# Weighted values a step later, inverses between GpSimd's folds: another order in a local attention loop

## The chip, the core and the metric

The kernel runs on one core of a Trainium2 chip. The metric is the device time of one execution in microseconds (us), the median of several runs; lower is better. All data are float32 unless said otherwise.

## The reference

A transformer block on x of 2 x 2048 x 256: attention with 16 heads of 16 in which each position sees itself and the 64 before it, a layer norm, a feed-forward layer in which each token goes to one of eight experts, and two more norms.

```python
qkv = x @ W_attn + b_attn                     # heads of 16
scores = einsum('bhtd,bhsd->bhts', q, k) * scale
mask = causal & (j >= i - 64)
attn = softmax(where(mask, scores, -inf), axis=-1)
out = einsum('bhts,bhsd->bhtd', attn, v)
x = layernorm(x + out @ W_proj + b_proj)

expert_idx = argmax(x @ Wr.T)                 # one expert of 8 for each token
inter = gelu(x @ W1[e] + b1[e])               # e = the token's expert
y = layernorm(inter @ Wo + bo + x) * gamma + beta
x = layernorm(x + y)
```

## The kernel before

The 4096 tokens are 32 tiles of 128. The first part of the kernel (to about 312 us of the span) is a loop over the tiles with one step for each tile; the second part runs the experts over blocks of 128 tokens that were sorted by expert, with gathered rows. The change lies in the first part and in the few lines that close it.

The order of the instructions on each engine is the order in which the program writes them: the loop is written out inside a manual schedule for TensorE, VectorE, ScalarE, GpSimd and the DMA queue of SyncE. Each engine works strictly down its own list, and semaphores that the tile framework sets hold an instruction back until its data are there, or until a buffer that it writes has been read.

A step `i` works on four tiles at once, each at another stage: `t = i`, `u = i - 1`, `w = i - 2`, `z = i - 3`.

- For `t`: `scores` (TensorE, L526 and L538) adds the mask and the products of queries and keys into four PSUM banks `s0` to `s3` of four heads each. `row_max` (VectorE, L550) takes each row's maximum of a bank, `exps` (ScalarE, L554) the exponentials, four instructions for each bank, into `pr`. `fold` (GpSimd, L566) adds the two halves of two banks' rows; with its second call it goes on to fold the sums in place three times, to widths 32, 16 and 8 (L574). The scores of the next step write the same four banks again.
- For `u`: `turn` (TensorE, L609) transposes the exponentials, a bank at a time, and `keep_turned` copies them out of PSUM into `pT`: banks 0 and 2 on ScalarE (L615), banks 1 and 3 on VectorE (L617). `pT` has one buffer. `weigh` (TensorE, L629, 64 matmuls) multiplies them with the values (`v` and `h`, the same values shifted by half a tile), and `keep_weighed` (ScalarE, L639) copies the result `pa` into `av`.
- For `w`: `inverse` (VectorE, L582 and L587) ends the row sums and inverts them, `spread_inverse` (GpSimd, L595) widens them to `rw`, `turn_inverse` (TensorE, L648) transposes that into PSUM, `normalise` (VectorE, L652) multiplies `av` with it, and `join` projects (TensorE, L660), adds the residual and takes the norm's statistics (VectorE, L666 to L670).
- For `z`: `norm_scale` (GpSimd, L676 and L677), `norm` (VectorE, L685, with the store to DRAM on SP's queue, L688), `turn_x1` (TensorE, L698) and `keep_x1` (ScalarE, L703). Every fourth step `route` (L710) and `turn_logits` (L720) take the router's logits of four tiles.

Between these stand two slots for the projection of later chunks of four tiles (`project`, L415 to L426, and `keep`, L462 to L492), by a table `work`; by it the steps repeat with a period of four (counted by `i` modulo 4). GpSimd adds the output bias to the residual at some steps (`add_bias`, L1111), and VectorE gets routing work at others.

Two kinds of PSUM buffers matter. Projections and `pa` share two banks in rotation (`psum`). All that is transposed, and `join`'s product, shares two others, taken in turn in the order of the calls:

```python
def turned(name):
    turns.append(name)
    return ps_t.tile([P, 4, P], F32, tag=f"pt{len(turns) % 2}", name=name)
```

so each such product waits until the one before the last has been read.

Of the kernel before, what the change touches and what calls it, by code (L numbers as in the profile page):

```python
# [17 lines left out]
P = 128  # L18
# [15 lines left out]
def kernel(  # L34
# [250 lines left out]
    with ExitStack() as att:  # L285
# [260 lines left out]
        def row_max(i, r):  # L546
            if r == 0:
                probs[i] = p2.tile([P, 4, 4, P], F32, tag="pr", name=f"pr_{i}", bufs=3)
                maxes[i] = small.tile([P, 4, 4], F32, tag="nm", name=f"nm_{i}")
            nc.vector.tensor_reduce(maxes[i][:, r, :], banks[i][r], AX.X, ALU.max, negate=True)  # L550

        def exps(i, r):
            for x in range(4):
                nc.scalar.activation(  # L554
                    probs[i][:, r, x, :], banks[i][r][:, x, :], AF.Exp,
                    bias=maxes[i][:, r, x : x + 1], scale=1.0,
                )

        def fold(i, pair):

            pr = probs[i]
            if pair == 0:
                sums[i] = p2.tile([P, NH, P // 2], F32, tag="fd", name=f"fd_{i}")
            fd = sums[i]
            two = slice(2 * pair, 2 * pair + 2)
            nc.gpsimd.tensor_tensor(  # L566
                fd[:, 8 * pair : 8 * pair + 8, :],
                pr[:, two, :, 0:CTX].rearrange("p r x c -> p (r x) c"),
                pr[:, two, :, CTX:P].rearrange("p r x c -> p (r x) c"), ALU.add,
            )  # L570
            if pair == 1:
                n = P // 4
                while n >= 8:
                    nc.gpsimd.tensor_tensor(  # L574
                        fd[:, :, 0:n], fd[:, :, 0:n], fd[:, :, n : 2 * n], ALU.add
                    )
                    n //= 2

        def inverse(i):

# [9 lines left out]
        def spread_inverse(i):  # L590

            ri = rTs.pop(i)
            rw = p2.tile([P, KC, 4, 2, HD], F32, tag="rw", name=f"rw_{i}")

            nc.gpsimd.tensor_copy(  # L595
                rw.rearrange("p g r o d -> p r g o d"),
                ri.rearrange("p (r g o) -> p r g o", r=4, g=KC).unsqueeze(4).to_broadcast(
                    [P, 4, KC, 2, HD]
                ),
            )  # L600
            rTs[i] = rw

        def turn(i, r):

            if r == 0:
                pTs[i] = p2.tile([P, 4, 4, P], F32, tag="pT", name=f"pT_{i}", bufs=1)
            pt = turned(f"pt_{i}_{r}")
            for x in range(4):
                nc.tensor.transpose(pt[:, x, :], probs[i][:, r, x, :], ident)  # L609
            pts[i, r] = pt  # L610
# [40 lines left out]
        def normalise(i):  # L651
            nc.vector.tensor_tensor(avs[i], avs[i], rTs.pop(i)[:, 0:KC, :], ALU.mult)  # L652
# [52 lines left out]
        def route(c):  # L705

            pl = turned(f"pl_{c}")
            for k in range(KC):
                for j in range(TPC):
                    nc.tensor.matmul(  # L710
                        pl[32 * j : 32 * j + 32, 0, :], lhsT=wrT[:, k, :], rhs=x1Ts[c][:, j, k, :],
                        start=(k == 0), stop=(k == KC - 1),
                    )
            lT = p2.tile([P, P], F32, tag="lT", name=f"lT_{c}", bufs=1)
            nc.scalar.copy(lT, pl[:, 0, :])
            x1Ts[c] = lT
# [484 lines left out]
        for i in range(NT):  # L1201


            t, u, w, z = (n if n >= 0 else None for n in range(i, i - 4, -1))
            slots = work[i]
            if w is not None:
                inverse(w)
            scores(t)
            if z is not None and z > 0 and z % TPC == 0:
                route(z // TPC - 1)  # L1210
            row_max(t, 0)
            if i == 0:
                consts = routing_constants()
                for r in range(1, 4):
                    row_max(t, r)
                for r in range(2):
                    exps(t, r)
                for n in ((0, 3), (1, 0), (1, 1)):
                    prepare(*n)
                for part in ((0, 3, 0), (0, 3, 1), (1, 0, 0), (1, 0, 1)):  # L1220
                    project(*part)
                    keep(*part)
                add_bias(0)
                xts[2] = load_x(2)
                for r in range(2, 4):
                    exps(t, r)
                for part in parts[:2]:
                    project(*part)
                    keep(*part)
                for pair in range(2):  # L1230
                    fold(t, pair)
                continue
            if i == 3:
                turn_router()
            if u is not None:
                turn(u, 0)
                keep_turned(u, 0)
                turn(u, 1)
            if z is not None:
                norm_scale(z)  # L1240
            if w is not None:
                spread_inverse(w)
            for part in slots:
                if part and part[2] == 0 and part[3][0] == 0:
                    prepare(*part[:2])
            exps(t, 0)
            row_max(t, 1)
            if u is not None:
                keep_turned(u, 1)

            full = slots[0] and slots[1] and slots[0][1] > 0 and slots[0][3] == (0, 1)
            if full:
                for task in early.get(i, ()):
                    task()
            if slots[0]:
                project(*slots[0])
            if i >= TPC + 3 and (i - 3) % TPC == 0:
                turn_logits((i - 3) // TPC - 1)

            light = not slots[0] or slots[0][3] == (0,)  # L1260
            if not light:
                exps(t, 1)
            row_max(t, 2)
            if slots[0]:
                row_max(t, 3)
            if u is not None:
                turn(u, 2)
                keep_turned(u, 2)
            if light:
                exps(t, 1)  # L1270
            if t < NT - 1:
                fold(t, 0)
            if i >= TPC - 1 and i % TPC in (0, TPC - 1):
                c = (i + 1) // TPC
                if c < NT // TPC:
                    add_bias(c, 2, 2 if i % TPC == 0 else 0)
                if i % TPC == 0 and c + 2 < NT // TPC:
                    xts[c + 2] = load_x(c + 2)
            for task in spread.get(i, ()):
                task()  # L1280
            if u is not None:
                turn(u, 3)
                keep_turned(u, 3)
            if not slots[0]:
                row_max(t, 3)
            if slots[0] and slots[0][3][-1] == 1:
                keep(*slots[0][:3])
            if z is not None:
                norm(z)
            exps(t, 2)  # L1290
            if slots[1]:
                project(*slots[1][:4])
            if w is not None:
                turn_inverse(w)
                normalise(w)
            if t == NT - 1:
                for b in range(2):
                    gather(b)
                inverse(u)
                spread_inverse(u)  # L1300
                quick_sums(t, 0)
            if not full:
                for task in early.get(i, ()):
                    task()
            if slots[1] and len(slots[1]) > 4:
                keep(*slots[1][:4])
            elif slots[1] and slots[1][3][-1] == 1:
                keep(*slots[1][:3])
            if u is not None:
                weigh(u)  # L1310
            exps(t, 3)
            if t < NT - 1:
                fold(t, 1)
            if u is not None:
                keep_weighed(u)
            if i == NT - 2:
                table(0)
            if z is not None:
                turn_x1(z)
                keep_x1(z)  # L1320

            if i == TPC:
                load_experts()
            if i == 2 * TPC:
                turn_biases()
            for task in plan.get(i, ()):
                task()
            if t == NT - 1:
                quick_sums(t, 1)
            if w is not None:  # L1330
                join(w)

# [5 lines left out]
            load_weights(n // PIECES, n % PIECES)  # L1340
        turn_in(0)
        keep_in(0)
        turn(u, 0)
        keep_turned(u, 0)
        turn(u, 1)
# [231 lines left out]
```

## Time and profile before

| | |
|---|---|
| runs | 584.68, 584.70, 584.93 us; median 584.7 |
| profiled execution | 585.55 us, span of its trace 583.7 us |
| TensorE clock granted, mean | 0.992 |
| busy in the span, us | TensorE 555.0, weight loads 452.0, VectorE 402.4, ScalarE 301.6, GpSimd 408.0 |
| busy from 120 to 150 us, of 30 | TensorE 29.65, weight loads 21.73, VectorE 26.69, ScalarE 20.91, GpSimd 22.06 |
| `exps` (L554) | 512 instructions, 142.2 us |
| `fold`, first adds (L566) | 62, 79.0 us |
| `fold`, in place (L574) | 93, 76.3 us |
| `keep_weighed` (L639) | 32, 372 to 523 ns |
| `norm` (L685) | 32, 328 to 1303 ns |

In the rows of the timeline the columns are the start in us from the span's start, the busy time in us, engine, line, operation, what is written and read with shapes, the number of instructions, and in brackets the engine's idle time before it with what ended it. PE is TensorE and PEld its weight loads, DVE VectorE, ACT ScalarE, POOL GpSimd, SP SyncE. Rows of one line that follow each other closely are merged into one. The ends of matmuls are modelled; their starts are recorded.

### The profile page before, as it was taken

How to read it: one execution, taken by the hardware profiler on the slowest of the kernel's cores; microseconds unless marked ns; L12 is line 12 of the kernel's file. 1: busy time of each engine (PE TensorE's matmuls, PEld its weight loads, DVE VectorE, ACT ScalarE, POOL GpSimd, SP SyncE). 2: the span in 40 equal slices, each digit the busy share in tenths (PEclk: the TensorE clock that was granted, in tenths of full speed). 3: DMA queues.
4: the chain of work that ended last, by engine and by line, in shares of the span. 5: the costliest groups of instructions: out<-in, count | busy, mean ns of one | idle time of the engine just before them, and what ended most of it. 6: DMA issues, size and time to landing. Idle time of an engine off the chain costs nothing.

```text
span 583.7 us, 18527 instructions
## 1 busy us (share of the span) xinstructions
PE 555.0 (95%) x7312; PEld 452.0 (77%) x7312; DVE 402.4 (69%) x966; ACT 301.6 (52%) x1005; POOL 408.0 (70%) x603
## 2 busy tenths in 40 slices
PE   8999999999999999999898999999999999999990
PEld 5658667676776767766666898999999999999880
DVE  5659788888988889989877567887863332232582
ACT  2487675776758577576765433233335455455100
POOL 5359777677787887868973488887878677652483
PEclk9999999999999999999999999999999999999996
DMA  5201603012030120211334454555555757754010
GB/s 162 86 2 46 177 25 96 21 45 79 11 104 21 46 76 12 56 30 58 90 105 127 165 181 172 182 182 181 181 194 188 261 180 246 252 160 153 19 39 27
DMA packets 35605, 64.79 MB, mean 111 GB/s; under 512 B 8558, under 2 KB 23484, under 8 KB 35516
## 3 DMA queue, kind: packets, MB, share of 16 engines
q1 hardware_dynamic: 32444, 55.19, 29.6%
q0 software_dynamic: 3072, 8.39, 4.5%
q8 instruction: 59, 0.97, 0.7%
q14 instruction: 30, 0.25, 0.1%
HBM read 48.93 MB, written 8.39 MB: 98 GB/s over the span
## 4 chain that ended last, share of the span: by engine, by line
PE 60%; POOL 14%; DVE 10%; ACT 6%; issue 3%; DMA 1%; POOLq 0%; DVEq 0%; ACTq 0%
PE ph L222 16%; PE py L242 14%; PE pt L609 6%; PE pj L419 4%; ACT pr L554 4%; PE pa L629 4%; PE py L660 4%; PE s L538 3%; POOL fd L574 3%; POOL fd L566 2%; PE pj L426 2%; DVE nm L550 2%; POOL row L849 2%; PE s L526 2%; POOL out_dram L274 1%
## 5 line engine op out<-in xcount | busy, mean ns | idle before, releaser
L554 ACT ACTIVATE pr<-s,nm 128x128 f32<-128x128 f32 x512 | 142.2, 416 | 6.9 <-DVE nm L550 5.9
L566 POOL TENSOR_TENSOR fd<-pr 128x512 f32<-128x512 f32 x62 | 79.0, 1274 | 64.6 <-ACT pr L554 64.6
L233 ACT ACTIVATE gT<-ph,bc 128x128 f32<-128x128 f32 x200 | 57.2, 370 | 107.5 <-issue 59.2
L222 PEld LDWEIGHTS ph<-xgT,wb 128*128 128x128 f32 x800 | 93.5, 192 | 1.3
L222 PE MATMUL ph<-xgT,wb 128*128 128x128 f32 x800 | 94.4, 275 | 0.0
L242 PE MATMUL py<-wo_sb,gT 128*128 128x256 f32 x400 | 90.6, 380 | 0.0
L550 DVE TENSOR_REDUCE nm<-s 128x4 f32<-128x512 f32 x128 | 82.0, 680 | 5.8 <-PE s L538 5.5
L574 POOL TENSOR_TENSOR fd<-fd 128x512 f32<-128x512 f32 (+2 forms) x93 | 76.3, 820 | 7.3
L242 PEld LDWEIGHTS py<-wo_sb,gT 128*128 128x128 f32 x400 | 74.1, 190 | 9.0
L609 PE MATMUL pt<-ident,pr 128*128 128x128 f32 x512 | 72.4, 281 | 3.8 <-DVE pT L617 1.6
L615 ACT COPY pT<-pt 128x512 f32<-128x512 f32 x64 | 38.5, 601 | 69.3 <-DVE nm L550 27.3
L609 PEld LDWEIGHTS pt<-ident,pr 128*128 128x128 f32 x512 | 55.4, 141 | 21.3 <-issue 9.7
L419 PE MATMUL pj<-xT,wa 128*128 128x512 f32 x128 | 60.6, 595 | 0.8 <-issue 0.8
L262 DVE TENSOR_TENSOR y<-py,xbo 128x256 f32<-128x256 f32 x32 | 13.5, 422 | 53.3 <-PE py L242 53.3
L617 DVE COPY pT<-pt 128x512 f32<-128x512 f32 x64 | 43.8, 684 | 6.6 <-PE pt L609 6.4
L538 PEld LDWEIGHTS s<-k,q 32*64 32x64 f32 x2048 | 30.8, 130 | 15.6 <-issue 15.0
L222 PE MATMUL ph<-xpT,wb 128*128 128x128 f32 x352 | 40.8, 275 | 0.0
L222 PEld LDWEIGHTS ph<-xpT,wb 128*128 128x128 f32 x352 | 40.1, 192 | 0.1
L538 PE MATMUL s<-k,q 32*64 32x128 f32 x2048 | 38.8, 278 | 0.4 <-DVE k L487 0.4
L272 DVE TENSOR_SCALAR res<-y,mv_c,rs_c 128x256 f32<-128x256 f32 x32 | 16.0, 499 | 28.9 <-POOL rs_c L256 23.9
L419 PEld LDWEIGHTS pj<-xT,wa 128*128 128x128 f32 x128 | 21.7, 190 | 17.6 <-issue 15.5
L255 POOL TENSOR_TENSOR rs_b<-mv_b,eps_ffn 128x1 f32<-128x1 f32 x32 | 9.2, 289 | 37.2 <-DVE mv_b L253 31.5
(235 smaller groups left out, 1005.5 us busy)
## 6 DMA issues: line engine op xcount, KB each, us to landing
wb<-in_L_ffn_W_dram SPq DMA_DIRECT2D x33, 1024.0 KB, 5.1
h<-v SPq DMA_DIRECT2D x24, 192.0 KB, 3.3
xt<-in_L_attn_x_dram SPq DMA_DIRECT2D x8, 512.0 KB, 4.9
x_d<-x SPq DMA_DIRECT2D x32, 128.0 KB, 1.7
wb<-in_L_ffn_W_dram SPq DMA_DIRECT2D x24, 128.0 KB, 2.2
h<-v SPq DMA_DIRECT2D x14, 96.0 KB, 2.7
wo_sb<-in_L_ffn_Wo_dram SPq DMA_DIRECT2D x1, 1024.0 KB
wa<-in_L_attn_W_attn_dram SPq DMA_DIRECT2D x3, 256.0 KB, 5.2
```

The costliest lines, as they stand in the source:

```text
L222: nc.tensor.matmul(phs[b, h][:, f % (NF // 2), :], lhsT=wb[:, k, ts(f, P)], rhs=xT[:, k, :], start=(k == 0), stop=(k == KC - 1),)
L233: nc.scalar.activation(gT[:, f, :], ph[:, f % (NF // 2), :], AF.Gelu, bias=bcs[b][:, f : f + 1], scale=1.0,)
L242: nc.tensor.matmul(py[:, 0:C], lhsT=gT[:, f, :], rhs=wo_sb[:, f, :], start=(f == 0), stop=(f == NF - 1),)
L419: nc.tensor.matmul(pm, lhsT=wa[:, k, ts(f, P)], rhs=axT[c][:, k, :], start=(k == 0), stop=(k == KC - 1),)
L538: nc.tensor.matmul(banks[i][r][a * CTX : (a + 1) * CTX, 2 * g + o, :], lhsT=qs[c][rows, g, o, t0 : t0 + CTX], rhs=ks[c][rows, g, t0 : t0 + P],
L550: nc.vector.tensor_reduce(maxes[i][:, r, :], banks[i][r], AX.X, ALU.max, negate=True)
L554: nc.scalar.activation(probs[i][:, r, x, :], banks[i][r][:, x, :], AF.Exp, bias=maxes[i][:, r, x : x + 1], scale=1.0,)
L566: nc.gpsimd.tensor_tensor(fd[:, 8 * pair : 8 * pair + 8, :], pr[:, two, :, 0:CTX].rearrange("p r x c -> p (r x) c"), pr[:, two, :, CTX:P]. ...
L574: nc.gpsimd.tensor_tensor(fd[:, :, 0:n], fd[:, :, 0:n], fd[:, :, n : 2 * n], ALU.add)
L609: nc.tensor.transpose(pt[:, x, :], probs[i][:, r, x, :], ident)
L615: nc.scalar.copy(pTs[i][:, r], pt)
L617: nc.vector.tensor_copy(pTs[i][:, r], pt)
```

## The change

In the loop's step, `weigh` no longer takes tile `u` near the step's end but tile `w` directly behind the next scores; `keep_weighed` follows behind the exponentials of bank 0. `turn_inverse` and `normalise` move ahead of the third turn, `join` ahead of `turn_x1`. On GpSimd the fold with the second pair of banks keeps only the first in-place add; the other two follow a step later behind `spread_inverse`, which itself goes ahead of `norm_scale`. Behind the loop, `weigh` and `keep_weighed` of the last but one tile are added. The same instructions are issued, 64 matmuls a tile for `weigh` as before, and no DMA more or less.

```diff
             if pair == 1:
-                n = P // 4
-                while n >= 8:
-                    nc.gpsimd.tensor_tensor(
-                        fd[:, :, 0:n], fd[:, :, 0:n], fd[:, :, n : 2 * n], ALU.add
-                    )
-                    n //= 2
+                fold_sums(i, P // 4)
+
+        def fold_sums(i, *widths):
+            fd = sums[i]
+            for n in widths:
+                nc.gpsimd.tensor_tensor(
+                    fd[:, :, 0:n], fd[:, :, 0:n], fd[:, :, n : 2 * n], ALU.add
+                )
...
             scores(t)
             if z is not None and z > 0 and z % TPC == 0:
                 route(z // TPC - 1)
+            if w is not None:
+                weigh(w)
             row_max(t, 0)
...
                 turn(u, 0)
                 keep_turned(u, 0)
                 turn(u, 1)
+            if w is not None:
+                spread_inverse(w)
+            if u is not None:
+                fold_sums(u, P // 8, P // 16)
             if z is not None:
                 norm_scale(z)
-            if w is not None:
-                spread_inverse(w)
...
             exps(t, 0)
+            if w is not None:
+                keep_weighed(w)
             row_max(t, 1)
             if u is not None:
                 keep_turned(u, 1)
...
             if i >= TPC + 3 and (i - 3) % TPC == 0:
                 turn_logits((i - 3) // TPC - 1)
+            if w is not None:
+                turn_inverse(w)
+                normalise(w)
...
             if slots[1]:
                 project(*slots[1][:4])
-            if w is not None:
-                turn_inverse(w)
-                normalise(w)
...
-            if u is not None:
-                weigh(u)
             exps(t, 3)
             if t < NT - 1:
                 fold(t, 1)
-            if u is not None:
-                keep_weighed(u)
             if i == NT - 2:
                 table(0)
+            if w is not None:
+                join(w)
             if z is not None:
                 turn_x1(z)
                 keep_x1(z)
...
                 quick_sums(t, 1)
-            if w is not None:
-                join(w)
...
         keep_in(0)
+        weigh(w)
+        keep_weighed(w)
         turn(u, 0)
```

## The prediction

> **What bounds the kernel now.** I read the page first, then TensorE's and ScalarE's timelines of one step, then the windows of four steps, then the queue orders of both programs. The change lies in the attention part, 26 to 312 us of the span, where the page shows TensorE busy in nearly every slice at the full clock:
>
> ```profile
> PE 555.0 (95%) x7312; PEld 452.0 (77%) x7312; DVE 402.4 (69%) x966; ACT 301.6 (52%) x1005; POOL 408.0 (70%) x603
> ...
> PE   8999999999999999999898999999999999999990
> ...
> PEclk9999999999999999999999999999999999999996
> ```
>
> So a step of the loop lasts as long as its matmuls. Step 12 on TensorE:
>
> ```profile
> 124.95 0.61 PE L526 MATMUL s<-m_b,m_a 64*128 64x512 bf16 x4
> 125.49 1.21 PE L538 MATMUL s<-k,q 32*64 32x128 f32 x64
> 126.62 1.09 PE L609 MATMUL pt<-ident,pr 128*128 128x128 f32 x8
> 127.56 0.60 PE L415 MATMUL pj<-ident,xt 128*128 128x128 f32 x4
> 128.00 1.23 PE L609 MATMUL pt<-ident,pr 128*128 128x128 f32 x8
> 129.06 1.89 PE L426 MATMUL pj<-wa,xT 128*128 128x256 f32 x8
> 130.79 0.38 PE L648 MATMUL pr<-ident,rw 128*128 128x128 f32 x2
> 131.11 0.43 PE L629 MATMUL pa<-pT,h 128*32 128x64 f32 x16
> ...
> 132.41 1.03 PE L660 MATMUL py<-wpj,av 128*128 128x256 f32 x4
> 133.37 0.60 PE L526 MATMUL s<-m_b,m_a 64*128 64x512 bf16 x3
> ```
>
> Starts follow each other without a hole, 8.42 us from scores to scores. ScalarE in the same step looks half idle, but see where the idle time lies:
>
> ```profile
> 127.36 0.59 ACT L615 COPY pT<-pt 128x512 f32<-128x512 f32 x1 [2.74 <-DVE nm L550]
> 127.85 2.18 ACT L554 ACTIVATE pr<-s,nm 128x128 f32<-128x128 f32 x8
> 129.86 0.65 ACT L615 COPY pT<-pt 128x512 f32<-128x512 f32 x1
> 130.32 2.26 ACT L554 ACTIVATE pr<-s,nm 128x128 f32<-128x128 f32 x8
> 132.34 0.51 ACT L639 COPY av<-pa 128x256 f32<-128x256 f32 x1
> 132.61 0.51 ACT L703 COPY x1T<-px 128x256 f32<-128x256 f32 x1
> ```
>
> It waits once, 2.74 us, for the first turned bank, and is then full until the last exponential ends at 132.58. The next scores write the banks that these exponentials read. "DVE nm" is only the last of several semaphores: the copy starts 0.74 us after its turn (126.62) here, and 0.73 to 0.74 in every undisturbed step, also where scores and turn lie elsewhere. So there is a loop scores, first turn, ScalarE's run, next scores, and it is shorter than the matmuls by little. From each step's scores the last exponential ends at 7.63 of 8.42 us (step 12), 8.88 of 9.49 (step 9), 8.12 of 8.41 (step 10), 8.33 of 10.27 (step 11). In step 2, where it is the bound, L538 starts 0.36 us after the exponentials' end instead of 0.54 after the step's start, so the period may be 0.18 us below that end. Slack: 0.97, 0.79, 0.47 and 2.12 us. These are the loop's four kinds of step, by i modulo 4: A (12), B (9), C (10), D (11).
>
> **The change part by part.** Offsets are from a step's first L526.
>
> 1. weigh goes from the step's end to behind the next scores: 64 matmuls and their loads, 1.03 us (131.11 to L698 at 132.14), no DMA. The first turn moves from 1.67 to 2.70, so ScalarE's run starts at 3.44 instead of 2.41 (in D, behind the routing product, 4.01 instead of 2.98). Its waits for v's writes and h's DMAs lie a step back then; v and h are rewritten two steps after it at the nearest, so nothing waits for their release.
>
> 2. keep_weighed leaves the end of ScalarE's run, where its 0.51 us were free, for a place between the exponentials of bank 0 and 1. Start to start it costs 0.28 us (132.34 to 132.61). With 1: the last exponential ends 1.31 us later, 0.34 over A's slack, 0.52 over B's, 0.84 over C's, none over D's.
>
> 3. turn_inverse and normalise go ahead of the third turn, and this costs more. The turns use two PSUM tiles in rotation, and the new order makes the fourth turn reuse the tile that turn_inverse filled. It needs normalise (VectorE), which needs keep_weighed (ScalarE), which stands behind bank 0's exponentials. On TensorE all of slot 1, join, turn_x1 and the next scores queue behind that turn; on VectorE the row maxima of banks 2 and 3, the fourth bank's copy and norm queue behind normalise.
>  - A and C: turn 2.70, copy 3.44, exponentials 3.92 (copy to exponential 0.48), keep_weighed 4.93 to 5.40, normalise 5.45 to 5.86 (its row: 0.41). From a copy's end on VectorE to the block behind the next turn the trace shows 0.55 (128.52 to 129.06, step 12): slot 1 at 6.40. Its eight matmuls 1.73, join 0.86, two transposes and the switch to the scores' shape 0.31 (0.96 behind L660 less its 0.86, plus 0.21): 9.30. C grows by 0.9.
>  - In A more comes: see norm below; 9.6, by 1.2.
>  - B: slot 0's projection stands first; turn_inverse at 5.35, normalise 0.5 later (0.49 and 0.54 where VectorE waited for it: steps 2, 28), to 6.26; slot 1 at 6.81 instead of 5.20. Its k copy (ScalarE, ahead of bank 3's exponentials) started 1.92 behind slot 1: 8.73; last exponential 0.58 later, to 10.49; less 0.18: 10.3, by 0.8.
>  - D: first turn 3.28, slot 0 from 4.21 to 5.94, logits' turn, turn_inverse 6.05, normalise 6.55 to 6.97, slot 1 at 7.5, join 9.24, end 10.4, by 0.15.
>
> 4. join goes ahead of turn_x1. TensorE loses the switches L648 to L629 (0.10 over the two matmuls) and L698 to L660 (0.06): 0.16 a step, contained in the sums above.
>
> 5. GpSimd: the same four operations, with the spread (0.40) now after the first in-place fold and the two small folds (0.74 and 0.46) behind it. The inverse is ready at about 2.6 to 3.3, turn_inverse comes at 4.1 or later: covered; late GpSimd would add directly to 3. SP's order does not change, and x1's store shifts with norm.
>
> norm (L685) runs beside GpSimd with very different times. In step 9 it took 0.41 us with GpSimd idle; in step 10 this:
>
> ```profile
> 111.42 1.27 POOL L566 TENSOR_TENSOR fd<-pr 128x512 f32<-128x512 f32 x1 [0.61 <-ACT pr L554]
> 111.54 1.30 DVE L685 TENSOR_SCALAR x<-xb,mv,rs 128x256 f32<-128x256 f32 x1
> ```
>
> It ends 0.15 us behind GpSimd's operation. The Trainium skill, "SBUF — State Buffer", section "SBUF: two separate sides", says that the two engines' shared port is an exclusive lock, the loser blocked for the whole instruction. In A, norm comes to 8.2, when GpSimd, with the fold at 6.45 and the bias add (1.33) behind it, is busy to 9.0: norm ends at 9.15, turn_x1 (0.17 behind it, as the turns after their copies) starts at 9.3, the step ends at 9.6. By the mean of L685 (0.7) turn_x1 would wait for nothing and A be 9.3, six times 0.3 less. I take the lock.
>
> A rule that speaks against the change: "TensorE: Matmul & The Clock Gate", section "A second HAM failure mode: psum-queue depth-cycling", says that short idle spells between groups made a kernel's clock fall back repeatedly. Half clock for 3.4 us in each of 30 steps would add some 50 us (estimate, from that page's window). But the trace granted 1.00 from 240 to 270 us, where TensorE was idle 2.0 of 30 us, and 1.00 from 300 to 330 with 3.3 idle; the change opens holes of some 1 us. I take nothing.
>
> **Sum.** Steps 4 to 23, five rounds of 1.2 + 0.8 + 0.9 + 0.15: 15.3. Step 24: 1.2. Step 8, where turn_biases now waits behind join's tile, 0.2; steps 13 and 17, where VectorE comes late from routing work, 0.1 each. Step 2 (like C, but held by the exponentials before) 1.1, step 3 0.9. Step 25 1.3 (VectorE is 2.5 us late there already, and A before it pushes it on). Steps 26 and 27, where three banks of exponentials stand behind the third turn, 1.0 each, as 1.31 less a slack of 0.2 to 0.3. Steps 28 to 30: 0.8, 0.5, 0.65. Step 31 and the tail: ScalarE's 1.3 late, weigh's 1.03 beside waits: 1.2. Together 25.4. The expert part behind it runs on TensorE and starts later by as much. The profiled execution, 585.55 us with a span of 583.7, would become 610.9; it lies 0.85 over the median, which goes from 584.7 to 610.
>
> **Rivals.** (a) Only the ScalarE loop counts, since the fourth turn's wait is filled by something I overlook: 0.34 + 0.52 + 0.84 a round, 8.5 for five, and about 8 for the other steps: 601. For it: the release is inferred from the rotation and not from a trace. (b) Faster: TensorE stays the bound, the saved switches (0.16 x 30 = 4.8) and weigh's former waits for VectorE's release of its bank (1.5) come off: 578.5. It needs a slack of 1.31 us in ScalarE's loop in each step; from there on it decides. D alone has it; against it stands the constant 0.74 between turn and copy. (c) No change: delay absorbed where VectorE is late anyway, switches making up the rest: 584 to 586. (d) Worse: VectorE, busy 8.1 of 8.42 us in A and C, loses its new waits for good and falls behind; another 0.4 us a step: 622.
>
> **Numbers.** Forecast 0.76 (its own range 604 to 616), (a) 0.10, (b) 0.04, (c) 0.02, (d) 0.08. The range 598 to 620 takes in (a) and part of (d). A change within 0.2%, 1.2 us, is about what a measurement of this kernel cannot tell from none: faster 0.04, same 0.02, slower 0.94.
>
> **What would show it.** Right: steps of some 9.6, 10.3, 9.3 and 10.4 us from L526 to L526; the first pT copy at 3.44; TensorE's L609 waiting for av, about 1 us in A and C; norm in A ending behind the bias add. Wrong: the first copy earlier than 0.7 us behind its turn; TensorE without holes; steps at 8.3.

## The result, and the profile after

The changed kernel takes 614.72 us, the median of four runs from 610.27 to 615.37, where the kernel before, run beside it, takes 584.77: a ratio of 1.0491 (95% interval 1.0472 to 1.0511). The profiled execution took 615.1 us with a span of 613.3, so the span is 29.5 us longer. The prediction said 610.0. A row keeps its work but not its line: L609 is now L611, L629 is L631, L639 is L641, L648 is L650, L652 is L654, L660 is L662, L666 is L668, L685 is L687, L698 is L700 and L1111 is L1113.

The page of the changed kernel has TensorE at 9 in fewer slices than before, and its clock row is no longer full: there is a 7 in the third slice and an 8 at 337 us.

```profile
PE   8989898999999999989877999999999999999990
...
PEclk9979999999999999999999899999999999999996
```

Step 12 (kind A) of the changed kernel, from the timeline of all engines, starts at 137.70:

```profile
137.70 0.60 PE L526 MATMUL s<-m_b,m_a 64*128 64x512 bf16 x4
...
140.40 1.09 PE L611 MATMUL pt<-ident,pr 128*128 128x128 f32 x8
141.14 0.59 ACT L617 COPY pT<-pt 128x512 f32<-128x512 f32 x1 [2.91 <-PE pt L611]
...
142.63 0.40 ACT L641 COPY av<-pa 128x256 f32<-128x256 f32 x1
...
143.06 0.42 DVE L654 TENSOR_TENSOR av<-av,pr 128x256 f32<-128x256 f32 x1 [0.77 <-ACT av L641]
...
143.54 0.66 PE L611 MATMUL pt<-ident,pr 128*128 128x128 f32 x4 [0.53 <-DVE av L654]
...
145.37 1.28 POOL L1113 TENSOR_TENSOR xb<-xt,bp_bc 128x512 f32<-128x512 f32 x1
...
145.79 1.01 DVE L687 TENSOR_SCALAR x<-xb,mv,rs 128x256 f32<-128x256 f32 x1
...
146.95 0.41 PE L700 MATMUL px<-ident,x 128*128 128x128 f32 x2 [0.16 <-DVE top L777]
...
147.29 0.60 PE L526 MATMUL s<-m_b,m_a 64*128 64x512 bf16 x4
```

Read it downwards as one chain. The first turn starts 2.70 us behind the scores instead of 1.67. Its copy follows at 3.44, keep_weighed at 4.93, normalise at 5.36, and only then may the fourth turn write its PSUM tile, after a hole of 0.53 us on TensorE. At the end norm takes 1.01 us beside GpSimd's bias add, and turn_x1 waits for it. The step is 9.59 us long; before it was 8.42. (The bracket names "top" L777 as the releaser, but it lies right behind norm on VectorE and turn_x1 reads norm's x.)

TensorE's waits, in us in total, how often, and the longest, put these causes high:

```profile
PE pt L611 <- DVE av L654: 9.1, 17, 0.6
PE px L700 <- DVE x L687: 3.8, 8, 0.9
PE s L526 <- ACT pr L554: 3.2, 8, 1.2
PE pt L611 <- issue: 2.2, 1, 2.2
```

In the kernel before, the first row stands at 0.2 us, once, the second is not in the list, and the third stands at 1.2 us, once. The fourth is a kind of stall that the prediction did not have: no semaphore ends it.

From L526 to L526 the changed steps 9 to 12 take 9.80, 9.79, 10.27 and 9.59 us. Of C's 9.79, 0.55 lies ahead of L538, which waits there for B's last exponential, so it belongs to B's loop. Counted so:

| kind of step | before | predicted | after |
|---|---|---|---|
| A | 8.42 | 9.6 | 9.59 |
| B | 9.49 | 10.3 | 10.3 |
| C | 8.41 | 9.3 | 9.24 |
| D | 10.27 | 10.4 | 10.27 |

So the repeating steps came out as worked out. By their starts alone, which is how the prediction worded its sign, B lies 0.5 us under its figure and C 0.5 over; their sum, 19.6, is the predicted one. The other 4.2 us of the span have to be looked for elsewhere.

| part of the span | predicted, us more | measured, us more |
|---|---|---|
| steps 1 to 3 | 2.0 | 4.46 |
| steps 4 to 24 | 16.9 | 18.11, of it 3.03 in two stalls without a semaphore (steps 5 and 8) |
| steps 25 to 30 | 5.25 | 4.58 |
| step 31 and the tail | 1.2 | 2.78 |
| ahead of step 1 | 0 | -0.39 |

The last row is scatter: step 1 starts between 25.75 and 26.52 us in the thirteen profiles of this document.

### The profile page after: what moved, and what is told of

It is laid out like the page before. It is cut to its first block, busy times and chain, and to the rows that moved or that the text cites. A ratio compares the mean times of both kernels' runs of the same rounds, so it can differ in the third digit from the quotient of the medians.

```text
span 613.3 us, 18522 instructions
## 1 busy us (share of the span) xinstructions
PE 565.4 (92%) x7311; PEld 458.0 (75%) x7312; DVE 399.1 (65%) x966; ACT 302.6 (49%) x1005; POOL 406.7 (66%) x603
## 4 chain that ended last, share of the span: by engine, by line
PE 33%; POOL 9%; DVE 6%; issue 2%; ACT 2%; DMA 1%; SPq 0%; POOLq 0%; DVEq 0%; ACTq 0%
PE ph L222 15%; PE py L242 14%; POOL row L851 1%; POOL out_dram L274 1%; PE pt L611 1%; POOL xg L150 1%; ACT pr L554 1%; PE pg L188 1%; PE pa L631 1%; POOL rs_b L256 1%; DVE x L687 1%; DMA xg<-x_d,g_idx_b 1%; POOL late_gT L1475 1%; POOL fd L566 1%; POOL xbo L180 1%
## 5 line engine op out<-in xcount | busy, mean ns | idle before, releaser
L554 ACT ACTIVATE pr<-s,nm 128x128 f32<-128x128 f32 x512 | 145.3, 415 | 4.8 <-DVE nm L550 4.5
L611 PE MATMUL pt<-ident,pr 128*128 128x128 f32 x512 | 77.2, 286 | 15.2 <-DVE av L654 9.1
L611 PEld LDWEIGHTS pt<-ident,pr 128*128 128x128 f32 x512 | 56.1, 143 | 30.5 <-DVE av L654 16.5
L538 PEld LDWEIGHTS s<-k,q 32*64 32x64 f32 x2048 | 31.5, 133 | 19.9 <-issue 18.9
L538 PE MATMUL s<-k,q 32*64 32x128 f32 x2048 | 39.6, 283 | 0.7 <-DVE k L487 0.7
L662 PE MATMUL py<-wpj,av 128*128 128x256 f32 x128 | 33.3, 382 | 0.4 <-ACT xgT L197 0.4
```

What stands on the lines that cost most here:

```text
L538: nc.tensor.matmul(banks[i][r][a * CTX : (a + 1) * CTX, 2 * g + o, :], lhsT=qs[c][rows, g, o, t0 : t0 + CTX], rhs=ks[c][rows, g, t0 : t0 + P],
L554: nc.scalar.activation(probs[i][:, r, x, :], banks[i][r][:, x, :], AF.Exp, bias=maxes[i][:, r, x : x + 1], scale=1.0,)
```

## Experiments

Times are medians; a ratio is to the kernel before, run on the same chip, which took 585.15, 585.25 and 585.37 us in the three sets (first: e1, e2, e3, e5; second: e4, e6, e7, e8; third: e9, e10, e11). Some put a part of the change alone into the kernel before, others alter the changed kernel.

| | us | ratio and 95% interval |
|---|---|---|
| e1_fill | 611.15 | 1.0446 (1.0427 to 1.0465) |
| e2_kw_first | 605.38 | 1.0348 (1.0332 to 1.0363) |
| e3_weigh_third | 601.44 | 1.0277 (1.0261 to 1.0293) |
| e5_weigh_back | 598.58 | 1.0227 (1.0211 to 1.0243) |
| e4_pool_only | 585.20 | 1.0002 (0.9994 to 1.0010) |
| e6_between | 585.16 | 1.0003 (0.9995 to 1.0012) |
| e7_join_only | 585.82 | 1.0014 (1.0003 to 1.0024) |
| e8_inverse_only | 601.12 | 1.0269 (1.0254 to 1.0284) |
| e9_weigh_only | 607.74 | 1.0384 (1.0368 to 1.0400) |
| e10_bias_early | 600.34 | 1.0250 (1.0234 to 1.0265) |
| e11_join_twice | 583.91 | 0.9977 (0.9967 to 0.9988) |

### e1_fill: is it the clock in step 2?

The changed kernel, with transposes of no use that keep TensorE busy while it waits for step 1's exponentials:

```diff
+            if i == 2:
+                for n in range(2):
+                    pw = turned(f"fill_{n}")
+                    for m in range(12):
+                        nc.tensor.transpose(pw[:, 0, :], ident, ident)
```

> The changed kernel with 24 more transposes of the identity ahead of the scores of step 2, in the place where TensorE now waits some 2.5 us for the exponentials of step 1. They cost nothing by themselves, since the exponentials set the start of the scores there. Theory (the hole of step 2 lets the clock fall to half for some 7 us): every run at 610.0 to 610.8 us with a mean clock of 0.99 or more, step 2 at about 10.5 us instead of 14.2. Rival (the spread from 610.3 to 615.4 has another cause, such as the 2.2 us that TensorE stands in step 5 without a wait): runs still spread to 613 and more. A second rival, that the transposes lie on the path: 2.6 us more, 612.9 in every run.

The windows of the changed kernel show what the change itself did there (columns: the window, its length, busy us and instruction counts of PE, PEld, DVE, ACT and POOL, then the granted clock, DMA share and GB/s):

```profile
31.30:36.30 5.00, 3.01 (x53) 1.61 (x60) 0.55 (x3) 3.11 (x11) 3.00 (x3) 0.75 0.00 0
36.30:41.30 5.00, 5.00 (x109) 4.39 (x94) 1.74 (x3) 1.32 (x5) 2.27 (x4) 0.56 0.01 3
...
337.00:342.00 5.00, 5.00 (x84) 4.66 (x85) 2.79 (x8) 1.36 (x4) 0.76 (x2) 0.66 0.50 148
```

With weigh gone from the end of step 1, TensorE waited 0.66 and then 1.24 us for exponentials, with only single matmuls between, and from about 33.8 to 40.7 us it was granted half its clock; the 64 score matmuls (L538) took 2.01 us for 1.21. Step 2 lasted 14.21 us. With the filling the same windows have the full clock:

```profile
31.30:36.30 5.00, 5.00 (x139) 3.96 (x141) 0.93 (x4) 2.83 (x10) 3.28 (x3) 1.00 0.00 0
36.30:41.30 5.00, 4.39 (x57) 3.20 (x46) 3.29 (x7) 3.91 (x13) 2.91 (x5) 1.00 0.03 7
```

Steps 1 and 2 together then take 17.21 us for 19.50; that is 2.3 of the 3.6 us by which the median falls. The spread did not vanish as expected: five runs from 610.41 to 613.31, with mean clocks of 0.992 to 0.987. In the profiled one (612.75) two other stretches, 294.7 to 298.1 and 335.6 to 339.0 us, ran at half clock. The second is the one that the changed kernel has at 337 us, behind two waits of 0.88 and 0.85 us close together: eight turns took 1.97 us for 1.09. That explains most of the tail's 1.6 us above the prediction: in the profile of e2_kw_first, which has the full clock there, step 31 and the tail take 1.3 us less, though with keep_weighed at another place. The four runs of the changed kernel fit: the one with a mean clock of 0.992 took 610.27 us, the other three, at 0.984 to 0.986, took 614.3 to 615.4.

### e2_kw_first: the wait of the fourth turn

e1_fill, with keep_weighed ahead of bank 0's exponentials:

```diff
+            if w is not None:
+                keep_weighed(w)
             if u is not None:
                 turn(u, 0)
                 keep_turned(u, 0)
...
             exps(t, 0)
-            if w is not None:
-                keep_weighed(w)
```

(On ScalarE the first place lies just ahead of the first turned bank's copy.)

> As the filled kernel, with the copy of the weighted values (ScalarE) ahead of the first turned bank's copy, where ScalarE stands idle, instead of behind bank 0's exponentials. Theory (its place costs twice: 0.28 us in ScalarE's run, and the wait of normalise, and so of the fourth turn, for it): normalise in steps A and C at about 4.7 us from the step's start instead of 5.4 and 5.4; A and C shorter by 0.3, B by 0.1, D by nothing, together 0.7 a round of four steps, 3.5 for five rounds and 1 for the others: 606. Rival (the weighted product ahead of the first turn alone sets the pace, since ScalarE's run begins there): no change within 0.7 us, 610. A second rival (turn_inverse itself, waiting for the spread or for the first bank's copy, takes the place of the copy): 609 to 610.

605.38 us: normalise comes earlier, slot 1 in A starts at 5.65 instead of 6.33 us, and 5.8 us of e1_fill's time go (5.4 between the runs of both with a mean clock of 0.992). C falls from 9.80 to 9.12 us; B stays, and D, for which nothing was expected, grows from 10.27 to 10.67 in steps 7 and 11. In A the step still takes 9.32, because turn_x1, whose turn would come at about 8.25, waits for norm until 8.97. That is what e10_bias_early takes up.

### e3_weigh_third: weigh behind two turns

e1_fill, with weigh behind the second turn instead of ahead of the first, which needs a second buffer for pT (and leaves two for pr):

```diff
-            if w is not None:
-                weigh(w)
...
                 turn(u, 0)
                 keep_turned(u, 0)
                 turn(u, 1)
             if w is not None:
+                weigh(w)
                 spread_inverse(w)
```

> As the filled kernel, with the weighted product behind the first two turns instead of ahead of them; the turned weights get two buffers and the exponentials two instead of three, so that nothing has to wait for a buffer. Theory (the 1.03 us ahead of the first turn are the largest part of A's and C's loss): first copy at 2.41 us from the step's start again, A about 8.6, C about 8.5, D 10.4, B still 10.3, since there the fourth turn waits for turn_inverse behind slot 0: 1.3 us a round over before, 594 in all. Rival (the wait of the fourth turn for normalise carries the loss, wherever weigh stands): A and C at 9.3 or more, 607 to 611.

Steps A and C behaved as expected (8.59, and 9.13 with 0.55 of it B's, the first copy back at 2.41), but 601.44 us is 7 more than expected. B and D came out some 0.2 us longer than expected, and in steps 13, 25 and 29, where VectorE comes late, the first turn waits 4.1 us in all. The timeline of step 13 shows for what:

```profile
141.37 1.09 PE L611 MATMUL pt<-ident,pr 128*128 128x128 f32 x8 [1.43 <-DVE xb L668]
```

With join's product ahead of turn_x1's in the rotation of the two tiles, the next step's first turn reuses join's tile and needs join's residual add on VectorE.

### e5_weigh_back: without weigh's move

The changed kernel with weigh and keep_weighed back at the end of the step before:

```diff
-            if w is not None:
-                weigh(w)
...
-            if w is not None:
-                keep_weighed(w)
...
+            if u is not None:
+                weigh(u)
             exps(t, 3)
...
+            if u is not None:
+                keep_weighed(u)
...
-        weigh(w)
-        keep_weighed(w)
```

> The changed kernel with weigh and its copy back at the end of the step before, as in the kernel before; turn_inverse and normalise ahead of the third turn, join ahead of turn_x1 and GpSimd's new order stay. Theory (without the copy behind bank 0's exponentials normalise is ready early; the fourth turn waits 0.45 to 0.55 us for it and the switch between shapes gives 0.3 back): A and C within 0.1 us of before, B and D longer by 0.15 each: 586.5 to 588. Rival (the place of turn_inverse carries most of the loss): 600 or more. A second rival, that the moved parts other than weigh are a gain and weigh alone a loss: under 584.

598.58 us: without weigh's move 16.1 us of the loss go (12.6 against e1_fill, where step 2's clock plays no part), but 13.4 us remain, and this expectation was far off. What remains is mostly the moved inverse, as e8_inverse_only confirms. In B (step 5) the fourth turn waits 0.36 us for normalise, and weigh then some 0.2 for a PSUM bank that VectorE reads late, since row maxima stand behind normalise on VectorE and the copy of slot 0's q behind those. Idle time ahead of weigh's instructions, in us and times; it counts the weight loads too, which run ahead of the matmuls, so not all of it is lost:

```profile
  DVE q L476: 5.8, 6
...
  DVE xT L464: 2.5, 6
```

In the kernel before, the same rows are 4.3 (9 times) and 1.0 (6). And the rotation shifts by one: the third turn now takes the tile that bank 1's copy on VectorE has to leave, 0.48 us behind turn_inverse where turn_inverse itself takes 0.22.

### e4_pool_only: GpSimd's part

In the kernel before, the second fold ends with its first in-place add (`fold_sums(i, P // 4)`), and further down:

```diff
-            if z is not None:
-                norm_scale(z)
             if w is not None:
                 spread_inverse(w)
+            if u is not None:
+                fold_sums(u, P // 8, P // 16)
+            if z is not None:
+                norm_scale(z)
```

> The kernel before with the GpSimd part of the change alone: the fold with the second pair of banks keeps one in-place add, the other two follow a step later behind spread_inverse, and that goes ahead of norm_scale. Theory of the prediction (this part is covered by TensorE's matmuls): 584.9 us, within 0.6 of the kernel before. Rival, the two small adds pushed a step on make VectorE's inverse of the next step late, and with it turn_inverse: 587 or more. Rival, the widened inverse comes earlier and a wait of turn_inverse goes: 583.5.

585.20 against 585.25: nothing lost, nothing gained.

### e6_between: is a switch of shape saved?

On top of e4_pool_only, in odd steps:

```diff
+            between = w is not None and slots[1] and i % 2 and slots[1][3] == (0, 1)
+            if between:
+                project(*slots[1][:3], (0,))
+                turn_inverse(w)
+                project(*slots[1][:3], (1,))
...
```

> The GpSimd part, and in the 14 odd steps (kinds B and D) turn_inverse put between the two halves of slot 1's projection, ahead of which it always had to switch shape to weigh. Where it counts: the two inverse transposes then have the projection's shape on both sides, and the switch from them to weigh (0.10 us) goes: 14 x 0.10 = 1.4 us, 583.4. Rival, its PSUM tile is not read out yet at that point (ScalarE's copy of bank 2 begins 5.55 us behind the step's start in B and 6.25 in D, the half slot ends at 6.05 and 6.82) and the transposes wait some 0.2 us each time: 586 to 588. Rival, the projection has a switch of its own behind them: no change, 584.9.

585.16 us, no change. The timeline of step 9 shows that the cost only changes place:

```profile
102.13 0.38 PE L650 MATMUL pr<-ident,rw 128*128 128x128 f32 x2
102.35 1.02 PE L419 MATMUL pj<-xT,wa 128*128 128x512 f32 x2
103.31 0.43 PE L631 MATMUL pa<-pT,h 128*32 128x64 f32 x16
```

The inverse now takes 0.22 instead of 0.32 from its start to the next, but the half slot ahead of weigh takes 0.96 instead of 0.86. Whichever of these two products stands ahead of weigh pays the 0.10. In the changed kernel weigh stands behind the scores, and there the 0.10 is saved, as the part on the prediction shows.

### e7_join_only: join ahead of turn_x1

In the kernel before:

```diff
+            if w is not None:
+                join(w)
             if z is not None:
                 turn_x1(z)
...
-            if w is not None:
-                join(w)
```

> The kernel before with one part of the change: join ahead of turn_x1. The prediction counted 0.06 us a step as saved: 583.5 us. Theory now: in the trace of the run with weigh put back, TensorE needs 1.03 (weigh) + 0.97 (join) + 0.32 (turn_x1 and switch) = 2.32 us from L629 to the next L526 against 1.03 + 0.27 + 0.96 = 2.26 before, so 0.06 is lost in each of 28 steps, 1.7 us; and the next step's first turn now reuses join's tile and waits for join's residual add on VectorE where VectorE is late (steps 13, 17, 25, 28), some 0.3 us each: together 588. A rival, that the wait for the residual add comes in all steps: 595 or more.

585.82 us, 0.14% more (interval 0.03 to 0.24), and not the 588 of the theory. The runs fall into two groups: eight of the fourteen took 584.8 to 585.9 us, as the kernel before does, and six 586.9 to 587.7 at a mean clock of 0.988 to 0.990. The profile is of the first group; where the second loses its time is not shown. In the profile the usual step is 0.05 longer, not shorter: from join's start directly behind weigh to the next start it is 0.97 us, and turn_x1 takes 0.31, where turn_x1 and join took 0.27 and 0.96. Two steps are much shorter, 8 (9.28 to 8.84) and 30 (8.48 to 8.00).

### e8_inverse_only: turn_inverse and normalise ahead of the third turn

The GpSimd part, and this in the kernel before:

```diff
+            if w is not None:
+                turn_inverse(w)
+                normalise(w)
...
             if slots[1]:
                 project(*slots[1][:4])
-            if w is not None:
-                turn_inverse(w)
-                normalise(w)
```

> The kernel before with turn_inverse and normalise ahead of the third turn and the GpSimd part; weigh, keep_weighed and join at their old places. Theory (normalise and, behind it, the row maxima of two banks hold up VectorE's keep of slot 0, and weigh at the step's end waits for the PSUM bank that this keep reads): about 0.35 us a step, the 598.6 us of the run with weigh put back less 3 for join, 595.5. Rival (only the fourth turn's wait for normalise counts, some 0.4 us a round of four steps): 587. Rival (join's place made the whole difference): 585.

601.12 us, 5.6 more than the theory, and more than e5_weigh_back, though join's change is left out. So join's new place, which loses 0.6 us by itself, wins 2.5 here. In A norm took 1.43 us (6.39 to 7.82) beside GpSimd's bias add (6.38 to 7.67), and turn_x1, directly behind weigh, started at 7.96 where weigh was done at 7.55; the step took 9.17, against 8.84 with join's 0.97 us between. TensorE waited 3.7 us for norm in nine places.

### e9_weigh_only: weigh and keep_weighed alone

```diff
+            if w is not None:
+                weigh(w)
             row_max(t, 0)
...
             exps(t, 0)
+            if w is not None:
+                keep_weighed(w)
...
-            if u is not None:
-                weigh(u)
...
-            if u is not None:
-                keep_weighed(u)
...
+        weigh(w)
+        keep_weighed(w)
```

The kernel before with these and e1_fill's transposes.

> The kernel before with weigh and keep_weighed a step on (behind the next scores, behind the exponentials of bank 0) and 24 transposes of no use in step 2 that keep TensorE busy there; turn_inverse, normalise and join stay at their old places, GpSimd as before. Theory: ScalarE's loop gets longer by 0.34, 0.52, 0.84 and 0 us in A, B, C and D, and join, which now stands some 1.3 us behind turn_inverse with only turn_x1 (0.27) between, waits for normalise in the steps where that is longer: some 2.4 us a round, 604. Rival, ScalarE's loop alone (the prediction's rival (a)): 601. Rival, no loss as long as turn_inverse is not moved: 586.

607.74 us, 3.7 above the theory and 6.7 above the rival. Its waits say that both were wrong on the cause:

```profile
PE px L698 <- DVE x L685: 13.6, 23, 1.3
PE py L660 <- DVE av L652: 1.7, 4, 0.6
```

No row has steady scores waiting for exponentials. turn_x1 waits for norm in 23 steps. In step 12 VectorE's copy of bank 1 starts at 3.90 us instead of 2.89, with 0.94 us of idle time ahead of it, and everything behind it on VectorE moves back by as much; norm starts 1.03 us later and, beside the bias add, takes 0.97 us instead of 0.70. The delay that opens on ScalarE by weigh's 1.03 us opens on VectorE too, and that engine had no room. This is read from the trace; no run took work off VectorE to test it. Steps A, B, C and D grew by 0.90, 0.65, 0.82 and 0.71 us.

### e10_bias_early: is it the lock?

e2_kw_first, with GpSimd's bias add put ahead of the first fold, where GpSimd is idle, in every fourth step from 4 to 28 (the six of kind A and step 28):

```diff
+            if i >= TPC and i % TPC == 0:
+                add_bias(i // TPC, 2, 2)
             if t < NT - 1:
                 fold(t, 0)
...
-                if c < NT // TPC:
+                if c < NT // TPC and i % TPC:
```

> The changed kernel with the filling transposes in step 2 and keep_weighed ahead of bank 0's exponentials (605.4 us in its own run), and GpSimd's add_bias (1.33 us) moved in six steps of kind A from behind the first fold to ahead of it, where GpSimd is idle. Theory (norm and GpSimd's add_bias exclude each other on the port, and turn_x1 waits for norm): turn_x1 in A starts at some 8.3 instead of 8.97 us behind the step's start, six times 0.7 us less: 601. Rival, norm is late for VectorE's own queue and its length in the trace is only what is recorded: no change, 605.4, A stays at 9.3. Rival, add_bias then delays the fold behind it and with it the inverse: 606 or more.

600.34 us, 5.0 less. Step 12 of it, starting at 129.47:

```profile
133.93 1.28 POOL L1113 TENSOR_TENSOR xb<-xt,bp_bc 128x512 f32<-128x512 f32 x1
...
136.89 0.40 DVE L687 TENSOR_SCALAR x<-xb,mv,rs 128x256 f32<-128x256 f32 x1
...
137.72 0.38 PE L700 MATMUL px<-ident,x 128*128 128x128 f32 x2
```

norm is back at 0.40 us, turn_x1 starts at 8.25 instead of 8.97, and A takes 8.56 instead of 9.32. The six steps of this kind give 4.7 of the 5.0; step 28 gives nothing (10.05 and 10.13).

### e11_join_twice: the part that pays

The kernel before, with join ahead of turn_x1 in steps 8 and 30 only:

```diff
+            join_first = i in (8, 30)
+            if join_first:
+                join(w)
             if z is not None:
                 turn_x1(z)
...
-            if w is not None:
+            if w is not None and not join_first:
                 join(w)
```

> The kernel before with join ahead of turn_x1 in two steps only, 8 and 30. In the trace of the run with join ahead in all steps these two alone were shorter (step 8 from 9.28 to 8.84 us, step 30 from 8.48 to 8.00), the others longer by some 0.05 each. Theory: 0.9 us less and nothing lost, 584.3 where the kernel before has 585.2. Rival, the gain is only moved on to the steps behind (9 and 31 wait for join's residual add): no change.

583.91 us, a ratio of 0.9977 (0.9967 to 0.9988) to the kernel before, so this beats both. In step 8 of the kernel before, join stood behind turn_x1 and turn_biases (L1098), and its tile had to be read by keep_x1 first:

```profile
95.71 1.13 PE L660 MATMUL py<-wpj,av 128*128 128x256 f32 x4 [0.40 <-ACT x1T L703]
```

With join first this hole is gone; step 8 takes 8.84 us, step 9 gives 0.09 back, step 30 takes 8.00 for 8.48. These account for 0.83 us of the 1.5 between the medians; the interval (0.7 to 1.9) holds both.

## Why the prediction was right, and where it was off

The sign, the size and the chain behind it were right: 610.0 predicted, 614.72 measured. Point by point:

- **weigh's place and ScalarE's run** (steps 1 and 2 of the prediction). The first turn at 2.70 and its copy at 3.44 are in the trace to the hundredth. But the worth of this move alone was mis-sized. Rival (a), in which only ScalarE's longer loop counts, came to 601 us; with weigh and keep_weighed moved alone the kernel takes 607.74, and its trace shows VectorE's delay, not ScalarE's, reaching TensorE. That this does not show in the sum of the whole change, because the fourth turn's wait takes its place, is argued and not shown.
- **The fourth turn's wait for normalise** (step 3). Shown: 9.1 us of waits in 17 places, and e2_kw_first takes 5.8 us off by bringing keep_weighed, and with it normalise, forward. Rival (a)'s doubt about the rotation is settled. The prediction looked for a hole of about 1 us in A and C; it is 0.53 in A. Another 0.26 lies behind turn_inverse (4.17 to 4.65 us behind the start of step 12, where turn_inverse itself takes 0.22), where the third turn waits for bank 1's copy, so slot 1 at 6.33 is still close to the 6.40 worked out.
- **The parts do not add.** Weigh alone costs 22.4 us (with the filling), the inverse 15.9, join 0.6 (between two groups of runs), GpSimd nothing: 38.8. Together, with the filling, they cost 26.0. A reading that fits: the two large parts delay the same engines' work at the same place in the step, and a hole on TensorE is paid once.
- **Switches saved** (step 4: "0.16 a step, contained in the sums above"). Right for the whole change, as far as its trace shows it. Step 9 of the changed kernel has no wait at these places:

```profile
113.29 0.38 PE L650 MATMUL pr<-ident,rw 128*128 128x128 f32 x2
113.51 1.40 PE L611 MATMUL pt<-ident,pr 128*128 128x128 f32 x8
...
116.47 1.03 PE L662 MATMUL py<-wpj,av 128*128 128x256 f32 x4
117.33 0.38 PE L700 MATMUL px<-ident,x 128*128 128x128 f32 x2
117.64 0.60 PE L526 MATMUL s<-m_b,m_a 64*128 64x512 bf16 x3
```

From its start to the next, turn_inverse takes 0.22 us for 0.32 before, and join and turn_x1 take 0.86 + 0.31 for 0.96 + 0.27; the scores take 1.14 to the next start and weigh 1.03, both as before. B without waits from outside (step 21) fits: the fourth turn takes 0.37 us more, 0.16 comes off, and the step goes from 9.49 to 9.71. The saving hangs on the neighbours: put into the kernel before, join stands directly behind weigh and loses 0.05 a step (e7_join_only), and a product put between turn_inverse and weigh takes the 0.10 over (e6_between). What the prediction did not count are join's waits: its new place covers norm (e8_inverse_only against e5_weigh_back), and it ties the next first turn to VectorE (e3_weigh_third).

- **GpSimd covered** (step 5): e4_pool_only, 585.20 against 585.25.
- **norm and the lock.** In A the prediction took the lock, 9.6, over the row's mean, 9.3. Measured 9.59, and e10_bias_early shows the cause by moving GpSimd's instruction away from norm. The rule that it cited of the Trainium skill, "SBUF — State Buffer", section "SBUF: two separate sides", agrees: norm takes 0.40 us alone and 1.01 to 1.43 beside the bias add (e10_bias_early, the changed kernel, e8_inverse_only), and ends 0.15 us behind it.
- **The clock** ("I take nothing"). This is the term that failed. The prediction weighed the Trainium skill, "TensorE: Matmul & The Clock Gate", section "A second HAM failure mode: psum-queue depth-cycling", for the 30 repeating steps, where it was right: 1.00 was granted from 96.6 to 156.6 us with TensorE idle for 4.3 of 60. It should have asked it of the two places where waits crowd, step 2 and the tail. Those cost 2.3 us (e1_fill's profile against the changed kernel's, steps 1 and 2) and most of the tail's 1.6.
- **Stalls without a semaphore**: 3.03 us in steps 5 and 8, in no sum. See the last section.
- Against these, the repeating steps were put 1.8 us too high, 0.75 of it D's 0.15 a round that did not come, and steps 25 to 30 0.7 too high. The misses are 2.46, 3.03 and 1.58 us up, 1.8, 0.7 and 0.4 down: 4.2 in all. That the sum lies so close is in part luck, since 7 us up and 3 down offset each other.
- **Rival (d)**, VectorE behind for good at 622: not so, A and C return to the same offsets in each round. Rivals (b) and (c) needed slack that is not there.

## What to carry to other kernels

An engine that looks 60 or 70% busy over the span can still have no room at the place where its input comes late: when an instruction is put ahead of the one that feeds two engines, follow the delay down both queues to what the bottleneck needs last, not only down the one that looks tight. When products share PSUM tiles in rotation, a move of any of them gives every later one another predecessor to wait for, in odd steps as well as the usual; list who reads each tile under the new order. And the losses of a change's parts, each measured alone, need not add up, nor does a part that loses in most places lose in each: join's move, a small loss in the other steps of the kernel before, was worth keeping in two. What a product costs depends on what stands ahead of it, so a saving that is real in one order can be missing when the same move is tried alone.

## What the runs showed of the hardware

- Short holes can halve TensorE's clock for longer than they last. In step 2 of the changed kernel, holes of 0.66 and 1.24 us with one matmul between were followed by about 6.9 us at half clock, and 24 filling transposes ahead of that step's scores prevented it. In the kernel before, one hole of 1.24 us there, with weigh close ahead of it, cost no clock, nor did a hole of 0.5 us in each 9.6 in the steady steps. The holes alone do not decide it: as the loop ends, two of 0.79 and 0.85 us, 0.4 us apart, were followed by 3.4 us at half clock in e10_bias_early's profile (324.8 to 328.2 us), and the same two by none in e2_kw_first's. What decides there is not shown.
- The kernels that have weigh's 64 loads and 64 matmuls directly behind the scores' as many (the changed one, e1, e2, e9, e10) have TensorE stalls that no semaphore ends, in weigh or just behind it, 0.5 to 3.0 us in all; the kernel before and the seven others have none there. The largest, 2.24 us, is in the list of waits above. In the trace's DMA records the instruction queue (59 packets of some 16 KB) has a packet from 66.8 to 68.2 us, and TensorE goes on 1.39 us behind its end; for the others it is 1.3 to 1.5 us behind such a packet's end. This fits an instruction supply that falls behind a dense run of short instructions. No run varied the supply itself, so the cause is argued, not shown.
- Ahead of weigh's narrower tiles there are 0.10 us when one of the 128*128 products, turn_inverse or the projection, precedes (e6_between). Behind the scores (32*64 tiles) weigh adds none: they take 1.14 us to the next start with weigh behind them as with a turn (step 9 of both kernels).
